# First token of three LSTMs in seven block products instead of four full ones per gate

## The chip, the cores and the metric

The kernel runs on one core of one Trainium2 chip. The metric is the time of one execution on the device in microseconds (us), as the median of several runs. The core has five engines that run side by side and meet at semaphores: TensorE (PE, matrix products, whose results land in PSUM), VectorE (DVE), ScalarE (ACT, activations and copies), GpSimd (POOL) and the queues of the DMA engines (SP issues them). Each engine takes its instructions in the order in which the program gives them, so an instruction that waits also holds up all that stand behind it.

## What is computed

The reference is a stack of four graph layers on x with 128 batches of 64 tokens and 256 channels, all in f32: a graph convolution with batch norm, a layer with two graph convolutions and four LSTMs, and two attention layers. The change lies in the LSTMs of the second layer:

```python
for p in range(1, MAX_SKIP + 1):                      # p = 1, 2, 3, 4
    nw = Tv // p                                      # 64, 32, 21, 16 windows
    wins = h[:, :nw * p, :].reshape(Bv * nw, p, Hd)   # each window has p tokens
    last = _lstm_last(Wih[p-1], Whh[p-1], bih[p-1], bhh[p-1], wins)
    h = h.at[:, jnp.arange(nw) * p + (p - 1), :].set(last.reshape(Bv, nw, Hd))

def step(carry, x_t):                                 # one token of a window
    h, c = carry
    g = x_t @ Wih.T + h @ Whh.T + bias
    i, f, gg, o = jnp.split(g, 4, axis=-1)
    c = sigmoid(f) * c + sigmoid(i) * tanh(gg)
    h = sigmoid(o) * tanh(c)
```

State and cell begin at zero, so the first token of a window needs neither Whh nor gate f: three gates (i, g, o), each of 256 output channels from 256 input channels. The LSTM with p = 1 has only that first token; "the longer LSTMs" are those with p = 2, 3 and 4.

## The kernel before

The batches go through the LSTMs in eight superchunks of 16 batches, so a superchunk has 512, 336 and 256 windows for p = 2, 3 and 4. Channels lie on the 128 partitions, windows along the columns; 256 channels are two halves. A gate is thus a product of 2 x 2 blocks of weights with 2 (input halves, k) x 2 (halves of the columns, j) blocks of data. All later tokens, and the LSTM with p = 1, already do this with seven block products in place of eight, after Strassen and Winograd: GpSimd or VectorE forms sums of data blocks (`differences`), the weights' sums were formed once, TensorE makes the seven products ("kinds" 1 to 7), and copies and adds from PSUM put them together. The first token of the longer LSTMs is done directly, with four products of the full number of columns for each gate. Gates are numbered 0, 1, 2, 3 for i, f, g, o.

The units of other work (graph convolutions of the next superchunks, residuals, norms for the attention that follows) are generators. They are advanced at marks between the parts of the LSTMs; the lists RESIDUAL, CONV, BEGUN, AHEAD, LATE give the mark for each unit. In one superchunk, marks 0 to 3 lie in the LSTM with p = 1, 4 to 7 in p = 2, 8 to 13 in p = 3, 14 to 21 in p = 4; the first two marks of a longer LSTM (4 and 5, 8 and 9, 14 and 15) lie within its first token and just behind it, and .5 stands for marks in the middle of a token.

```python
    def differences(engine, dst, b11, b12, b21, b22, third=None):
        t1, t2, t3, t4 = dst
        return [lambda: engine.tensor_tensor(t1, b12, b11, OP.subtract),
                lambda: ((third or engine).tensor_tensor(t3, b22, b12, OP.subtract),
                         engine.tensor_tensor(t2, b22, t1, OP.subtract)),
                lambda: engine.tensor_tensor(t4, b21, t2, OP.subtract)]
    # ... cut ...
    # (weight set: blocks 0-3 are the four 128x128 blocks of Wih, 8-10 three of Whh; 4-7 and 11-14 their sums)
    BLOCKS = {1: (0, 8), 2: (2, 9), 3: (7, 14), 4: (3, 10), 5: (4, 11), 6: (5, 12), 7: (6, 13)}
    # ... cut ...
    def operands_x(p, hv, name, s):
        nw, nb, inner, tokens = columns_x(p, hv)
        m = nw * nb // 2
        t = l1.tile([P, 7 * (T // 3) * NB], F32, tag="xd", name=f"xd_{name}_{s}", bufs=2)
        t = [t[:, i * m : (i + 1) * m].rearrange("p (a b) -> p a b", b=inner) for i in range(4)]
        b = {(k, j): tokens(k, s, j) for k in range(KD) for j in range(2)}
        for f in differences(nc.gpsimd, t, b[0, 0], b[0, 1], b[1, 0], b[1, 1]):
            f()
        return {5: t[0], 6: t[1], 7: t[2], 4: t[3], 1: b[0, 0], 2: b[1, 0], 3: b[1, 1]}
    # ... cut ...
        gates = l1.tile([P, 4, KD, CH], F32, tag="gates", name=f"gates_{name}", bufs=1)
        cells = l1.tile([P, KD, CH], F32, tag="cell", name=f"cell_{name}", bufs=1)
        hn = l1.tile([P, KD, CH], F32, tag="hs", name=f"hs_{name}", bufs=1)
        hd = l1.tile([P, 4, CH // 2], F32, tag="hd", name=f"hd_{name}", bufs=1)
    # ... cut ...
        dh = differences(nc.vector, [hd[:, i, :m] for i in range(4)], b[0, 0], b[0, 1], b[1, 0], b[1, 1])
        oh = {i: folded(a) for i, a in {1: b[0, 0], 2: b[1, 0], 3: b[1, 1], 4: hd[:, 3, :m],
                                        5: hd[:, 0, :m], 6: hd[:, 1, :m], 7: hd[:, 2, :m]}.items()}
        ox = {1: x1}
        banks = {(q, c): bank(f"g{q}_{name}_{c}", tag) for q, tag in ((0, "y"), (2, "z"), (3, "x"))
                 for c in range(KD)}
        def first_acts(*qs):
            for q in qs:
                for c in range(KD):
                    nc.scalar.activation(
                        columns_of(gate(q, c)),
                        natural(banks[q, c][:, :n].rearrange("p (w b) -> p w b", b=nb)),
                        AF.Tanh if q == 2 else AF.Sigmoid, bias=bs[:, q * KD + c : q * KD + c + 1])
        def first_cell(c):
            nc.vector.tensor_mul(cells[:, c, :n], gate(0, c), gate(2, c))
            nc.scalar.activation(gate(2, c), cells[:, c, :n], AF.Tanh)
        products = [(q, c, k) for k in range(KD) for q in GATES[:3] for c in range(KD)]
        for at, (q, c, k) in enumerate(products):
            if at == 6:
                yield
            nc.tensor.matmul(
                banks[q, c][:, :n].rearrange("p (w b) -> p w b", b=nb), wsets[p, q][:, 2 * k + c, :],
                hv[:, k, : (nw - 1) * p + 1 : p, :], start=(k == 0), stop=(k == KD - 1))
        first_acts(0, 2)
        first_cell(0)
        first_acts(3)
        first_cell(1)
        for c in range(KD):
            new_state(0, c, every)
            if not c:
                dh[0]()
        dh[1]()
        dh[2]()
    # ... cut ...
        class Unit:
            def __init__(self, q, s):
                self.q, self.s = q, s
                self.banks, self.of = {}, {1: "x", 6: "x", 7: "x", 4: "x", 5: "y", 2: "z", 3: "z"}
            def psum(self, kind):
                return self.banks[self.of[kind]][:, m:n] if kind == 3 else self.banks[self.of[kind]][:, :m]
            def product(self, kind, parts="xh"):
                tag = self.of[kind]
                for part in parts:
                    first = tag not in self.banks
                    if first:
                        self.banks[tag] = bank(f"{tag}{self.q}_{name}_{self.s}", tag)
                    i = "xh".index(part)
                    nc.tensor.matmul(folded(self.psum(kind)), wsets[p, self.q][:, BLOCKS[kind][i], :],
                                     (ox[self.s] if part == "x" else oh)[kind], start=first,
                                     stop=(part == "h"), skip_group_check=True)
            def copy(self, kind):
                nc.scalar.copy(gate(self.q, kind // 5, halves[kind // 5]), self.psum(kind))
            def add(self, dst, a, kind):
                nc.vector.tensor_add(gate(self.q, *dst), gate(self.q, *a), self.psum(kind))
            def c11(self):
    # ... cut ...
            def c12(self):
    # ... cut ...
        A = [Unit(q, 1) for q in (0, 2)]
        each(A, pe(5, "x"), pe(3, "x"), pe(2, "x"))
        yield
        for s in range(1, p):
            last = s == p - 1
            B = [Unit(q, s) for q in (1, 3)]
            if not last:
                ox[s + 1] = operands_x(p, hv, name, s + 1)
            each(A, pe(5, "h"), do("copy", 5), pe(1), do("copy", 1), pe(3, "h"), pe(2, "h"), pe(6), do("u4"),
                 do("c11"), do("c12"))
            each(B[:1], pe(5), do("copy", 5))
            each(A, pe(7), do("c22"), do("act", 0))
            each(B[1:], pe(5), do("copy", 5))
            each(A, pe(4), do("act", 2), do("act", 1))
    # ... cut ...
    def ahead(c):
        yield from to_pairs(c)
        stats = ln_stats(xs[c], f"n2_{c}")
        yield
        h = l1r.tile([P, NJ, D], F32, tag="g", name=f"h2_{c}", bufs=3)
        yield from apply_halves(h, xs[c], stats, f"n2_{c}")
        mid = l1r.tile([P, Q, CH * KD // Q], F32, tag="g", name=f"nm_{c}", bufs=3)
        channel_squares(mid, h)
        far2[c] = put(mid, f"n2{c}", tag=f"n2{c}", bufs=1)
        yield
    # ... cut ...
    RESIDUAL = (0, 3, 4), (2, 5, 5.5)
    CONV = (3, 4, 4, 5, 5.5, 7, 8, 9, 10, 10), (3, 4, 4, 11, 11.5, 13, 14, 15, 15.5, 17, 18, 20)
    BEGUN = (11, 11, 13, 14, 16), (17, 17.5, 21)
    FIRST = (1, 2, 3, 3, 4, 4, 5, 5.5, 7, 8, 9, 10, 10), (1, 2, 4, 5, 6, 8, 11, 11.5, 13, 14, 15, 15.5, 17, 18, 20)
    AHEAD = (4, 5, 7, 12, 14, 19), (6, 7)
    LATE = 5, 6, 8, 9
    IDLE = {5: 4, 7: 18, 9: 10, 13: 14, 15: 8}
    FINAL = (4, 5, 9.5, 10, 12, 13), (6, 7, 11.5, 14, 14, 15)
    # ... cut ...
    banks_of("psum1", x=2, y=2, z=2, ps=2)
```

## Time and profile before

| what | value |
|---|---|
| time, median of 3 runs | 1868.78 us (1867.98 to 1869.43) |
| span of the profiled execution | 1866.5 us |
| PE busy, all products | 1844.3 us, 99% |
| DVE, ACT, POOL busy | 1251.4, 1013.4, 554.1 us |
| products of the first tokens of the longer LSTMs (line L1126) | 576 records, 184.1 us |
| activations that read these products (L1113) | 144, 75.2 us |
| products of all later tokens (L1155) | 5,376 records |
| weight sets of the longer LSTMs, loaded | 96 of 960 KB |

A line of the costliest groups reads: source line, engine, operation, tile written and tiles read, shape, number of instructions, busy time, mean in ns, idle time of that engine ahead of them and what ended it. A line of the timeline reads: start in us, duration, engine, source line, operation, tiles, shape, count; in brackets the idle time ahead and the engine that ended it. An f32 product appears as two records. The end of a matmul is modelled, so distances between starts tell more of TensorE than durations. A granted clock of 0.999 shows that TensorE was not throttled.

### The profile page before, as it was taken

How to read it: one execution, taken by the hardware profiler on the slowest of the kernel's cores; microseconds unless marked ns; L12 is line 12 of the kernel's file. 1: busy time of each engine (PE TensorE's matmuls, PEld its weight loads, DVE VectorE, ACT ScalarE, POOL GpSimd, SP SyncE). 2: the span in 40 equal slices, each digit the busy share in tenths (PEclk: the TensorE clock that was granted, in tenths of full speed). 3: DMA queues.
4: the chain of work that ended last, by engine and by line, in shares of the span. 5: the costliest groups of instructions: out<-in, count | busy, mean ns of one | idle time of the engine just before them, and what ended most of it. 6: DMA issues, size and time to landing. Idle time of an engine off the chain costs nothing.

```text
span 1866.5 us, 39078 instructions
## 1 busy us (share of the span) xinstructions
PE 1844.3 (99%) x15077; PEld 1476.6 (79%) x15077; DVE 1251.4 (67%) x3150; ACT 1013.4 (54%) x2284; POOL 554.1 (30%) x704
## 2 busy tenths in 40 slices
PE   8999989999999999999999999999999999999998
PEld 6877855996897798699589689878969967777776
DVE  5767856567467666667766756766566567776776
ACT  5766635556456455555654645655565534444453
POOL 5865712123213212212322311222132114322332
PEclk9999999999999999999999999999999999999999
DMA  3223652234334433333433443343144254544433
GB/s 115 70 63 143 236 206 64 91 128 166 108 119 150 155 130 131 120 116 116 153 119 120 164 153 119 142 132 123 62 140 152 64 159 137 153 142 143 142 114 114
DMA packets 111273, 241.45 MB, mean 129 GB/s; under 512 B 11504, under 2 KB 74864, under 8 KB 111088
## 3 DMA queue, kind: packets, MB, share of 16 engines
q1 hardware_dynamic: 110192, 237.09, 37.8%
q8 instruction: 119, 1.95, 0.4%
q0 software_dynamic: 320, 1.05, 0.2%
q10 hardware_dynamic: 576, 0.82, 0.1%
q14 instruction: 66, 0.54, 0.1%
HBM read 170.50 MB, written 68.42 MB: 128 GB/s over the span
## 4 chain that ended last, share of the span: by engine, by line
PE 90%; DVE 5%; ACT 2%; issue 1%; POOL 1%; DMA 1%; SPq 0%; DVEq 0%; ACTq 0%; POOLq 0%
PE x L1155 22%; PE z L1155 11%; PE g L1126 9%; PE y L1155 6%; PE v L1580 5%; PE x L1340 4%; PE y L1340 3%; PE u L929 3%; PE v L915 3%; PE p_q L1587 3%; PE X L1776 3%; PE X L423 2%; PE X L499 2%; PE Y L423 1%; PE Y L1776 1%
## 5 line engine op out<-in xcount | busy, mean ns | idle before, releaser
L1155 PE MATMUL x<-xd,wset 128*128 128x128 f32 (+2 forms) x1152 | 255.6, 304 | 1.4 <-DVE gates L1164 1.4
L1155 PE MATMUL x<-hd,wset 128*128 128x128 f32 (+2 forms) x1152 | 254.6, 303 | 0.0
L1221 POOL TENSOR_TENSOR gates<-gates 128x512 f32<-128x512 f32 (+2 forms) x48 | 75.1, 1565 | 497.1 <-ACT gates L1084 497.1
L1084 ACT ACTIVATE gates<-gates,bias 128x256 f32<-128x256 f32 (+4 forms) x384 | 172.5, 488 | 90.3 <-DVE gates L1164 90.3
L1164 DVE TENSOR_TENSOR gates<-gates,x 128x128 f32<-128x128 f32 (+2 forms) x384 | 120.9, 321 | 149.5 <-PE x L1155 146.5
L1164 DVE TENSOR_TENSOR gates<-gates,z 128x128 f32<-128x128 f32 (+2 forms) x384 | 102.4, 318 | 146.2 <-PE z L1155 146.2
L1155 PEld LDWEIGHTS x<-xd,wset 128*128 128x128 f32 x1152 | 187.8, 191 | 7.5 <-DVE gates L1164 2.6
L1155 PEld LDWEIGHTS x<-hd,wset 128*128 128x128 f32 x1152 | 187.9, 191 | 4.9
L1126 PE MATMUL g<-hT,wset 128*128 128x256 f32 (+2 forms) x576 | 184.1, 474 | 0.1
L1126 PEld LDWEIGHTS g<-hT,wset 128*128 128x128 f32 x576 | 108.7, 190 | 68.1 <-issue 38.0
L1161 ACT COPY gates<-y 128x128 f32<-128x128 f32 (+2 forms) x192 | 54.0, 292 | 196.3 <-PE y L1155 194.4
L1155 PE MATMUL z<-hs,wset 128*128 128x128 f32 (+2 forms) x768 | 146.6, 303 | 0.2 <-DVE hs L1093 0.2
L1155 PE MATMUL z<-hT,wset 128*128 128x128 f32 (+2 forms) x768 | 146.5, 303 | 0.0
L1155 PEld LDWEIGHTS z<-hs,wset 128*128 128x128 f32 x768 | 117.3, 191 | 3.9 <-DVE hs L1093 0.6
L1155 PEld LDWEIGHTS z<-hT,wset 128*128 128x128 f32 x768 | 117.2, 191 | 3.4
L1113 ACT ACTIVATE gates<-g,bias 128x512 f32<-128x512 f32 (+2 forms) x144 | 75.2, 560 | 40.5 <-PE g L1126 39.8
L1084 ACT ACTIVATE gates<-x,bias 128x128 f32<-128x128 f32 (+2 forms) x192 | 74.8, 390 | 29.7 <-PE x L1155 26.5
L1155 PE MATMUL x<-hT,wset 128*128 128x128 f32 (+2 forms) x384 | 86.0, 306 | 0.0
L1155 PE MATMUL x<-hs,wset 128*128 128x128 f32 (+2 forms) x384 | 84.9, 303 | 0.0
L1236 ACT ACTIVATE gates<-cell 128x256 f32<-128x256 f32 (+2 forms) x144 | 55.2, 383 | 47.5 <-DVE cell L1235 47.5
L1155 PE MATMUL y<-hd,wset 128*128 128x128 f32 (+2 forms) x384 | 79.3, 309 | 0.0
L1595 POOL TENSOR_TENSOR s<-s,mx 128x256 f32<-128x256 f32 (+2 forms) x33 | 40.4, 1225 | 128.1 <-DVE mx L1594 120.3
(326 smaller groups left out, 4170.4 us busy)
## 6 DMA issues: line engine op xcount, KB each, us to landing
wset<-wfar SPq DMA_DIRECT2D x96, 960.0 KB, 6.4
hT<-far_h SPq DMA_DIRECT2D x124, 128.0 KB, 3.2
far_h<-hm SPq DMA_DIRECT2D x16, 512.0 KB, 2.8
far_n<-xs SPq DMA_DIRECT2D x16, 512.0 KB, 3.4
xs<-far_n SPq DMA_DIRECT2D x64, 128.0 KB, 4.4
far_x<-xs SPq DMA_DIRECT2D x16, 512.0 KB, 3.0
x<-far_x SPq DMA_DIRECT2D x64, 128.0 KB, 3.2
xt<-in_x_dram SPq DMA_DIRECT2D x15, 512.0 KB, 4.2
```

The lines of the kernel that those rows point to most:

```text
L423: nc.tensor.matmul(self.banks[tag][:, i * CH // 2 : (i + 1) * CH // 2], w, self.at[kind], start=first and not i, stop=True, skip_group_che ...
L915: nc.tensor.matmul(banks[m], wg0_sb[:, k, m * P : (m + 1) * P], agg[:, k, :], start=(k == 0), stop=(k == KD - 1))
L929: nc.tensor.matmul(banks[j // 2][:, j % 2, :], v[:, k, j * P : (j + 1) * P], wg1_sb[:, k, :], start=(k == 0), stop=(k == KD - 1))
L1084: nc.scalar.activation(gate(q, c, part), src, AF.Tanh if q == 2 else AF.Sigmoid, bias=bs[:, q * KD + c : q * KD + c + 1])
L1113: nc.scalar.activation(columns_of(gate(q, c)), natural(banks[q, c][:, :n].rearrange("p (w b) -> p w b", b=nb)), AF.Tanh if q == 2 else AF. ...
L1126: nc.tensor.matmul(banks[q, c][:, :n].rearrange("p (w b) -> p w b", b=nb), wsets[p, q][:, 2 * k + c, :], hv[:, k, : (nw - 1) * p + 1 : p, ...
L1155: nc.tensor.matmul(folded(self.psum(kind)), wsets[p, self.q][:, BLOCKS[kind][i], :], (ox[self.s] if part == "x" else oh)[kind], start=firs ...
L1164: nc.vector.tensor_add(gate(self.q, *dst), gate(self.q, *a), self.psum(kind))
L1221: nc.gpsimd.tensor_mul(gates[:, 0, :, :n], gates[:, 0, :, :n], gates[:, 2, :, :n])
L1340: nc.tensor.matmul(folded(ps(g, kind)), wih1[:, g, KINDS1[kind], :], right[kind], start=kind in (2, 5, 1), stop=True, skip_group_check=True)
L1580: nc.tensor.matmul(ps[:, i, :], hT[:, k, j, :], w[:, k, first : first + D], start=(k == 0), stop=(k == KD - 1))
L1776: nc.tensor.matmul(st[c, tag][:, i * CH // 2 : (i + 1) * CH // 2].rearrange("p (a n) -> p a n", n=P), w, st[c, "o7"][kind], start=first an ...
```

## The change

The first token of each longer LSTM is now done in seven block products for each gate, with half the columns each. That asks for the data sums of token 0 as well as of token 1 (`operands_x`, on GpSimd, now for both at the end of the LSTM before), and so for a third buffer of these sums. Product 1 is copied out, as is product 5; the others are added or read by an activation. Both copies follow their products in the program at once, and the activation of the first channel half follows the last add to it. One block of the weight sets, no longer read, is dropped (14 blocks in place of 15). The first product with a token's sums of kind 5 in the second token moves behind the mark, so that it stands with its partner for h. The norms of the attention for the first chunk of each superchunk move one superchunk later, as those of the second chunk already were, and other units move to other marks. The purpose is to take products from TensorE.

The diff, cut to what the working needs:

```diff
--- before.py
+++ after.py
@@ -1021,7 +1021,7 @@
-    BLOCKS = {1: (0, 8), 2: (2, 9), 3: (7, 14), 4: (3, 10), 5: (4, 11), 6: (5, 12), 7: (6, 13)}
+    BLOCKS = {1: (0, 7), 2: (1, 8), 3: (6, 13), 4: (2, 9), 5: (3, 10), 6: (4, 11), 7: (5, 12)}
     def columns_x(p, hv):
         nw, nb = hv.shape[2] // p, hv.shape[3]
@@ -1040,14 +1040,14 @@
         nw, nb, inner, tokens = columns_x(p, hv)
         m = nw * nb // 2
-        t = l1.tile([P, 7 * (T // 3) * NB], F32, tag="xd", name=f"xd_{name}_{s}", bufs=2)
+        t = l1.tile([P, 2 * CH], F32, tag="xd", name=f"xd_{name}_{s}", bufs=3)
         t = [t[:, i * m : (i + 1) * m].rearrange("p (a b) -> p a b", b=inner) for i in range(4)]
         b = {(k, j): tokens(k, s, j) for k in range(KD) for j in range(2)}
         for f in differences(nc.gpsimd, t, b[0, 0], b[0, 1], b[1, 0], b[1, 1]):
             f()
         return {5: t[0], 6: t[1], 7: t[2], 4: t[3], 1: b[0, 0], 2: b[1, 0], 3: b[1, 1]}
-    def lstm(p, hv, name, follows, x1, ending):
+    def lstm(p, hv, name, follows, ox, ending):
         nw, nb, inner, tokens = columns_x(p, hv)
@@ -1103,37 +1103,51 @@
         dh = differences(nc.vector, [hd[:, i, :m] for i in range(4)], b[0, 0], b[0, 1], b[1, 0], b[1, 1])
         oh = {i: folded(a) for i, a in {1: b[0, 0], 2: b[1, 0], 3: b[1, 1], 4: hd[:, 3, :m],
                                         5: hd[:, 0, :m], 6: hd[:, 1, :m], 7: hd[:, 2, :m]}.items()}
-        ox = {1: x1}
-        banks = {(q, c): bank(f"g{q}_{name}_{c}", tag) for q, tag in ((0, "y"), (2, "z"), (3, "x"))
-                 for c in range(KD)}
-        def first_acts(*qs):
-            for q in qs:
-                for c in range(KD):
-                    nc.scalar.activation(
-                        columns_of(gate(q, c)),
-                        natural(banks[q, c][:, :n].rearrange("p (w b) -> p w b", b=nb)),
-                        AF.Tanh if q == 2 else AF.Sigmoid, bias=bs[:, q * KD + c : q * KD + c + 1])
-        def first_cell(c):
-            nc.vector.tensor_mul(cells[:, c, :n], gate(0, c), gate(2, c))
-            nc.scalar.activation(gate(2, c), cells[:, c, :n], AF.Tanh)
-        products = [(q, c, k) for k in range(KD) for q in GATES[:3] for c in range(KD)]
-        for at, (q, c, k) in enumerate(products):
-            if at == 6:
-                yield
-            nc.tensor.matmul(
-                banks[q, c][:, :n].rearrange("p (w b) -> p w b", b=nb), wsets[p, q][:, 2 * k + c, :],
-                hv[:, k, : (nw - 1) * p + 1 : p, :], start=(k == 0), stop=(k == KD - 1))
-        first_acts(0, 2)
-        first_cell(0)
-        first_acts(3)
-        first_cell(1)
-        for c in range(KD):
-            new_state(0, c, every)
-            if not c:
-                dh[0]()
+        class First:
+            def __init__(self, q, tags):
+                self.q, self.ps = q, [bank(f"{t}{q}_{name}_{i}", t) for i, t in enumerate(tags)]
+            def psum(self, kind):
+                return self.ps[kind in (5, 3)][:, m:n] if kind in (2, 3) else self.ps[kind in (5, 3)][:, :m]
+            def product(self, kind):
+                nc.tensor.matmul(folded(self.psum(kind)), wsets[p, self.q][:, BLOCKS[kind][0], :], ox[0][kind],
+                                 start=kind in (1, 5), stop=True, skip_group_check=True)
+            def copy(self, c, j, kind):
+                nc.scalar.copy(gate(self.q, c, halves[j]), self.psum(kind))
+            def add(self, dst, a, kind):
+                nc.vector.tensor_add(gate(self.q, dst[0], halves[dst[1]]),
+                                     gate(self.q, a[0], halves[a[1]]), self.psum(kind))
+        firsts = [First(q, tags) for q, tags in ((0, "yz"), (2, "yz"), (3, "xx"))]
+        def all_first(*fs):
+            for f in fs:
+                for u in firsts:
+                    f(u)
+        def made(kind):
+            return lambda u: u.product(kind)
+        all_first(made(1), lambda u: u.copy(0, 0, 1), made(5), lambda u: u.copy(1, 1, 5))
+        yield
+        all_first(made(2), lambda u: u.add((0, 0), (0, 0), 2), made(3), made(6), lambda u: u.add((0, 1), (1, 1), 6),
+                  made(7), lambda u: u.add((1, 1), (1, 1), 7), lambda u: u.add((0, 1), (0, 1), 3), made(4),
+                  lambda u: act(u.q, 0, every, gate(u.q, 0)))
+        nc.vector.tensor_mul(cells[:, 0, :n], gate(0, 0), gate(2, 0))
+        nc.scalar.activation(gate(2, 0), cells[:, 0, :n], AF.Tanh)
+        all_first(lambda u: act(u.q, 1, halves[1], gate(u.q, 1, halves[1])),
+                  lambda u: act(u.q, 1, halves[0], u.psum(4)))
+        new_state(0, 0, every)
+        dh[0]()
+        yield "a"
+        nc.vector.tensor_mul(cells[:, 1, :n], gate(0, 1), gate(2, 1))
+        nc.scalar.activation(gate(2, 1), cells[:, 1, :n], AF.Tanh)
+        new_state(0, 1, every)
         dh[1]()
         dh[2]()
@@ -1201,14 +1215,14 @@
             return lambda u: getattr(u, f)(*a)
         A = [Unit(q, 1) for q in (0, 2)]
-        each(A, pe(5, "x"), pe(3, "x"), pe(2, "x"))
+        each(A, pe(3, "x"), pe(2, "x"))
         yield
         for s in range(1, p):
             last = s == p - 1
             B = [Unit(q, s) for q in (1, 3)]
             if not last:
                 ox[s + 1] = operands_x(p, hv, name, s + 1)
-            each(A, pe(5, "h"), do("copy", 5), pe(1), do("copy", 1), pe(3, "h"), pe(2, "h"), pe(6), do("u4"),
+            each(A, pe(5, "h" if s > 1 else "xh"), do("copy", 5), pe(1), do("copy", 1), pe(3, "h"), pe(2, "h"), pe(6), do("u4"),
                  do("c11"), do("c12"))
             each(B[:1], pe(5), do("copy", 5))
             each(A, pe(7), do("c22"), do("act", 0))
@@ -1420,7 +1433,7 @@
         def ending(p):
             if p < SKIP:
-                operands[p + 1] = operands_x(p + 1, hv, names[p + 1], 1)
+                operands[p + 1] = {s: operands_x(p + 1, hv, names[p + 1], s) for s in range(2)}
             elif sc < NCH // SUP - 1:
                 nxt = hTs[sc + 1].rearrange("p k (t b) -> p k t b", t=T)
                 operands[1] = block_sums(blocks(sc + 1, nxt), f"{sc + 1}_1")
@@ -1482,14 +1495,14 @@
-    RESIDUAL = (0, 3, 4), (2, 5, 5.5)
-    CONV = (3, 4, 4, 5, 5.5, 7, 8, 9, 10, 10), (3, 4, 4, 11, 11.5, 13, 14, 15, 15.5, 17, 18, 20)
-    BEGUN = (11, 11, 13, 14, 16), (17, 17.5, 21)
-    FIRST = (1, 2, 3, 3, 4, 4, 5, 5.5, 7, 8, 9, 10, 10), (1, 2, 4, 5, 6, 8, 11, 11.5, 13, 14, 15, 15.5, 17, 18, 20)
-    AHEAD = (4, 5, 7, 12, 14, 19), (6, 7)
-    LATE = 5, 6, 8, 9
+    RESIDUAL = (0, 3, 5.5), (2, 5, 8.5)
+    CONV = (3, 4, 5, 5.5, 7, 8, 9, 10, 10), (5, 6, 9.5, 11, 11.5, 13, 14, 15, 15.5, 17, 18, 20)
+    BEGUN = (11, 11, 14.5, 17, 19, 21), (17.5, 19, 21)
+    FIRST = (1, 2, 3, 3, 4, 4, 5, 5.5, 7, 8, 9, 10, 10), (1, 2, 4.5, 5, 6, 9.5, 11, 11.5, 13, 14, 15, 15.5, 17, 18, 20)
+    AHEAD = (6, 7), (9, 10)
+    LATE = (4.5, 5.5, 9, 9.5), (9, 11, 12, 19.5)
     IDLE = {5: 4, 7: 18, 9: 10, 13: 14, 15: 8}
-    FINAL = (4, 5, 9.5, 10, 12, 13), (6, 7, 11.5, 14, 14, 15)
+    FINAL = (6, 7, 11, 12, 15, 15.5), (9, 10, 15, 16, 17, 17.5)
     START = (0, 1, 0, 0, 0, 1, 0, 1, 1, 0, 0, 1, 1, 0, 1, 2, 2)
     tc.no_sync_barrier()
@@ -1526,8 +1539,6 @@
                     todo.setdefault(n, []).append(unit)
-            if sc > 1:
-                units(LATE[:1], aheads[sc * SUP - 3])
             if sc < last:
                 for i in range(SUP):
                     units((CONV if sc else FIRST)[i], convs[(sc + 1) * SUP + i])
 ... cut: the block dropped from the weight sets; block_sums gets the same new buffers; both places that call units with LATE ...
```

## The prediction

> **What bounds the kernel now.** I read the page first: engine totals, chain, groups.
>
> ```profile
> span 1866.5 us, 39078 instructions
> ## 1 busy us (share of the span) xinstructions
> PE 1844.3 (99%) x15077; PEld 1476.6 (79%) x15077; DVE 1251.4 (67%) x3150; ACT 1013.4 (54%) x2284; POOL 554.1 (30%) x704
> ...
> PE 90%; DVE 5%; ACT 2%; issue 1%; POOL 1%; DMA 1%; SPq 0%; DVEq 0%; ACTq 0%; POOLq 0%
> ...
> L1126 PE MATMUL g<-hT,wset 128*128 128x256 f32 (+2 forms) x576 | 184.1, 474 | 0.1
> ```
>
> TensorE is the bound, and the products to be replaced (L1126, tile g) are 184 us of its time. Busy time does not say whether PE has slack, since ends of matmuls overlap and are modelled. So next I read the timeline of PE by start times, in the first tokens of one superchunk with p = 2, 3 and 4 (each product is two records, so x24 is 12 products):
>
> ```profile
> 603.17 5.31 PE L1126 MATMUL g<-hT,wset 128*128 128x512 f32 x12
> 608.41 1.16 PE L214 MATMUL agg_b<-adjt_bd,cv 64*64 64x64 f32 x64
> 609.50 5.42 PE L1126 MATMUL g<-hT,wset 128*128 128x512 f32 x12
> 614.76 1.03 PE L1155 MATMUL y<-xd,wset 128*128 128x256 f32 x4
> ...
> 645.82 6.94 PE L1126 MATMUL g<-hT,wset 128*128 128x336 f32 x24
> 652.60 0.73 PE L1155 MATMUL y<-xd,wset 128*128 128x168 f32 x4
> 653.17 1.30 PE L1155 MATMUL z<-hT,wset 128*128 128x168 f32 x8
> 654.40 1.16 PE L214 MATMUL agg_c<-adjt_bd,cv 64*64 64x64 f32 x64
> 655.49 0.84 PE L1155 MATMUL y<-hd,wset 128*128 128x168 f32 x4
> ...
> 690.53 5.34 PE L1126 MATMUL g<-hT,wset 128*128 128x256 f32 x24
> 695.71 0.61 PE L1155 MATMUL y<-xd,wset 128*128 128x128 f32 x4
> ```
>
> Start to start, a product of 336 columns takes (652.60-645.82)/12 = 0.565 us, one of 256 takes (695.71-690.53)/12 = 0.432. Other rows give 0.858 for 512, 0.285 for 168 (656.17, 656.45, 656.74) and 0.223 for 128. That is 1.65 ns a column plus about 11 ns, and no gap: the rows stand end to end. PE has almost no slack to hide a new wait in, and almost no old wait to lose. From one superchunk's start to the next is 153.5 us, and the starts show about 1.3 us of it lost in waits.
>
> **What the Trainium skill says.** "TensorE: Matmul & The Clock Gate", section "Back-to-back issue gap", makes the gap of warm matmuls N/2.4 + 2.5 ns. Per record our 112, 143, 216 and 429 ns are twice the N/2.4 part plus about 5 ns for these f32 products: the linear shape agrees, so narrow products cost no penalty here, though each weight load shows as 191 ns. "VectorE: DVE Perf Modes", section "The TRN2 errata", gives an f32 tensor_tensor as (N+151)/0.96 ns: 691, 424, 332 and 291 ns for 512, 256, 168, 128. The trace has 687, 420, 327 and 283, so of every small add about 155 ns is fixed. "PSUM — Partial Sum Buffer", section "PSUM bank collisions raise a hardware error", asks that PSUM be guarded by bank and quadrant, not by address. No run shows the error itself, but the changed program's waits follow that: product 2, which writes the second half of bank y, waits for ScalarE's copy of the first half.
>
> **The change, part by part.** First, PE. Before, per superchunk: 12 products of 512, 336, 256 columns = 12 x (0.858+0.565+0.432) = 22.26 us. After: 7 x 3 = 21 products of half the width = 21 x (0.432+0.285+0.223) = 19.74. Saved: 2.5 us a superchunk, 20 us in eight, 1.1% of the time. This is the ceiling of the gain.
>
> Second, the other engines. The seven products must be added up. For each p VectorE gets 12 adds from PSUM (0.42, 0.33, 0.28 us): 12 x 1.03 = 12.4 us a superchunk on top of 104.4 busy of 153.5. ScalarE loses 6 wide activations and gets 6 copies, 3 wide and 6 half ones, about 9 us on top of 86.4. GpSimd gets 4 differences for each p (0.73, 0.54, 0.45): 7 us on top of 37. None becomes the bound by load. Weight sets shrink from 960 to 896 KB; no wait for them stands in the chain, so nothing from that.
>
> Third, latency, where PE waits in order. I followed the changed order of instructions with the durations of the trace. From a product's end to the add's start is 0.27 us, other hand-overs are about 0.06.
>
> (a) Start of a token. The gates tile has one buffer, so the first copy waits for the previous LSTM's last state on VectorE, and product 2 waits for that copy. Before, products of the first input half took long enough to cover it.
>
> ```profile
> 604.63 0.65 DVE L1350 TENSOR_TENSOR gates<-gates 128x512 f32<-128x512 f32 x1
> 605.20 0.68 DVE L1356 TENSOR_TENSOR hT<-hs,gates 128x512 f32<-128x512 f32 x1
> 606.05 1.20 DVE L1356 TENSOR_TENSOR hT<-cell,gates 128x512 f32<-128x512 f32 x1 [0.16 <-ACT gates L1353]
> ...
> 646.10 0.99 DVE L1099 TENSOR_TENSOR hT<-gates 128x256 f32<-128x256 f32 x2
> ```
>
> For p=2 the state is there at 607.25. The aggregation (1.16) now stands ahead of the token, then products 1 and 5 take 6 x 0.432, so PE would be at product 2 at 603.17+1.16+2.6 = 606.9. The copy ends at 607.3+0.37, so PE starts at 607.7: 0.8 us lost. For p=3 and 4 a block of 3.4 us (u, v) stands ahead of the token; states come at 647.0 and 690.95, products 2 are due at 645.82+1.71 = 647.5 and 690.53+1.34 = 691.9: nothing lost.
>
> (b) Inside: products 6, 7 and 4 of a gate share one bank half, so each waits for the add of the one before, with two other gates between. For p=4, three products are 0.67 us and one round trip is 0.22+0.27+0.28+0.06 = 0.83: 0.16 lost twice, 0.3. For p=3 0.1 each, 0.2. For p=2 three products are 1.3: nothing.
>
> (c) End: the next token's product 5 needs bank y, which ScalarE frees only after three wide gates, one tanh, three half gates and then the half gate from that bank. For p=3: the last product 4 starts near 651.7, adds of product 3 end 651.9 to 652.5, three gates (0.5 apart) 653.5, tanh 654.1, four half gates 655.5. PE needs 1.14 for its four ready products and 1.2 for the aggregation, so it is there at 654.3: 1.2 lost. For p=2 and 4, v or u (3.4 us) stands there and covers it. Also for p=3, VectorE does the moved norm statistics (2.1 us) just ahead of the next token's adds: up to 0.7 more, which I count half.
>
> Sum of new waits a superchunk: 0.8 + 0.2 + 1.2 + 0.35 + 0.3 = 2.85 us. The last superchunk has no convolutions to fill waits of p=2 and p=4: some 3 us more. The norms that leave p=4 take statistics and activations out of the way of an old wait of 0.4 us there (below), which should go in most superchunks: -2.5 us.
>
> ```profile
> 712.51 0.49 PE L1155 MATMUL x<-xd,wset 128*128 128x128 f32 x2 [0.24 <-DVE gates L1164]
> ```
>
> Total: -20 + 8 x 2.85 + 3 - 2.5 = +3 us by this count. Each wait is worked out from VectorE and ScalarE running strictly in order; my errors are of 0.5 us a place, or some 6 to 10 us together, and my count takes every coincidence at its worst, though the units were moved (marks 5.5, 8.5, 14.5) so as to stay behind the first state. I therefore take 4 us off: **1868 us**.
>
> **Rivals.** The first: the waits are hidden, and all 20 us arrive, giving 1849. For it: PE's rows are so dense that the author clearly places fillers well, and only p=3 lacks one. Against it: the aggregation is 1.2 us, and the chain of (c) is 3.5. The second: VectorE becomes the bound in p=3 and p=4, because 12 adds more, slowed by GpSimd, fall into 4 us. For it: two tensor_tensor of 336 columns took 1.62 us instead of 1.0 at 651.68, while GpSimd worked there until 652.9. Against it: VectorE's load goes only from 68% to 76%. That would cost 1 to 1.5 us more a superchunk: 1878. The third: the transfers of weights, smaller now, start earlier and help. No wait for them is visible, so 0.
>
> **Range and chances.** The best case is 1849 plus a little, as some wait is sure: 1852. The worst has both later rivals' costs and a poor last superchunk: 1883. Over 2% faster (1831) is beyond the ceiling of the PE count; over 2% slower (1906) needs 7 us of waits a superchunk. So 0.01, 0.96, 0.03.
>
> **What would show it.** PE's product rows should have starts 0.432, 0.285, 0.223 apart; 504 products in place of 288. A gap ahead of product 2 for p=2 released by ScalarE's copy; a gap ahead of bank y's product in the second token of p=3, about 1.2 us, released by ScalarE; small ones inside p=4 released by VectorE's adds. Superchunks near 153.7 us apart. If they are 151 apart, (a) and (c) were hidden and I am wrong by some 20 us; if 155 or more, VectorE's queue is the cause.

## The result, and the profile after

The changed kernel takes **1896.66 us** (median of 4 runs, 1896.2 to 1897.3) against 1869.11 us (1867.98 to 1869.78) of the kernel before on the same chip. The ratio is 1.0148 with a 95% interval of 1.0131 to 1.0166: 27.5 us slower. I had predicted 1868 us with a range of 1852 to 1883; the time lies above it, on the side of the waits.

The page of the kernel after, the lines that answer to those shown of before (engine totals, chain by engine, and the group with the most idle time ahead of it on TensorE):

```profile
span 1894.5 us, 40708 instructions
...
PE 1840.2 (97%) x15509; PEld 1515.4 (80%) x15509; DVE 1325.8 (70%) x3438; ACT 1053.0 (56%) x2500; POOL 600.1 (32%) x800
...
PE 79%; DVE 11%; ACT 5%; issue 2%; POOL 2%; DMA 1%; SPq 0%; DVEq 0%; ACTq 0%; POOLq 0%
...
L1169 PE MATMUL x<-xd,wset 128*128 128x128 f32 (+2 forms) x1152 | 256.6, 304 | 12.4 <-ACT gates L1175 10.1
```

By the page TensorE is busy 4 us less (busy time counts modelled ends; the starts give more, see the table of terms below), and the span is 28 us longer. In the chain TensorE falls from 90% to 79%: the end is now set in part by VectorE and ScalarE. Neither is full; VectorE went from 67% to 70%. The last row is the first surprise: 10.1 us of waits in the *later* tokens' products (L1169, in the code of before L1155), of which the change only moves the first ones of the second token, for ScalarE's copies L1175.

The timeline of TensorE in superchunk 2, the first tokens with p=2, 3 and 4 and the tokens behind them (in square brackets the idle time ahead of a row and what ended it):

```profile
612.23 1.13 PE L1116 MATMUL y<-hT,wset 128*128 128x256 f32 x4 [0.56 <-ACT gates L1120]
...
657.58 1.16 PE L214 MATMUL agg_c<-adjt_bd,cv 64*64 64x64 f32 x64
659.62 0.52 PE L1169 MATMUL y<-xd,wset 128*128 128x168 f32 x2 [0.89 <-ACT gates L1084]
...
665.20 0.55 PE L1169 MATMUL x<-xd,wset 128*128 128x168 f32 x2 [0.21 <-DVE gates L1178]
...
736.07 0.46 PE L1169 MATMUL x<-xd,wset 128*128 128x128 f32 x2 [1.40 <-ACT gates L1175]
```

The first three waits stand where the prediction put them. Taken start to start, as the excess over the usual distance of two records, they are 0.72, 1.04 and 0.37 us. The fourth, 1.56 us in the last token of p=4, I had not seen.

The same by the matmuls' starts (first product of an LSTM to first product of the next, us), for superchunk 2, which stands for the steady ones, and for the last:

| | p=1 and 2 | p=3 | p=4 | superchunk 2 | superchunk 7 | behind the LSTMs |
|---|---|---|---|---|---|---|
| before | 60.68 | 44.71 | 48.13 | 153.52 | 143.06 | 371.1 |
| after | 60.27 | 45.98 | 49.25 | 155.49 | 153.35 | 375.4 |

The whole difference of the two profiled spans, 28.0 us, is: start -0.5, superchunk 0 +3.5, superchunks 1 to 6 +10.4, superchunk 7 +10.3, and the attention stage behind the LSTMs, which the change does not touch, +4.3.

### The profile page after: what moved, and what is told of

It is laid out like the page before. It is cut to its first block, busy times and chain, and to the rows that moved or that the text cites. A ratio compares the mean times of both kernels' runs of the same rounds, so it can differ in the third digit from the quotient of the medians.

```text
span 1894.5 us, 40708 instructions
## 1 busy us (share of the span) xinstructions
PE 1840.2 (97%) x15509; PEld 1515.4 (80%) x15509; DVE 1325.8 (70%) x3438; ACT 1053.0 (56%) x2500; POOL 600.1 (32%) x800
## 4 chain that ended last, share of the span: by engine, by line
PE 79%; DVE 11%; ACT 5%; issue 2%; POOL 2%; DMA 1%; SPq 0%; DVEq 0%; ACTq 0%; POOLq 0%
PE x L1169 20%; PE z L1169 10%; PE v L1592 5%; PE y L1169 5%; PE y L1116 4%; PE u L929 3%; PE v L915 3%; PE y L1353 3%; PE X L1788 3%; PE p_q L1599 3%; PE x L1353 2%; PE X L423 2%; PE x L1116 2%; PE X L499 2%; PE z L1116 1%
## 5 line engine op out<-in xcount | busy, mean ns | idle before, releaser
L1084 ACT ACTIVATE gates<-gates,bias 128x256 f32<-128x256 f32 (+4 forms) x528 | 237.8, 495 | 204.0 <-DVE gates L1178 109.0
L1169 PE MATMUL x<-xd,wset 128*128 128x128 f32 (+2 forms) x1152 | 256.6, 304 | 12.4 <-ACT gates L1175 10.1
L1169 PE MATMUL x<-hd,wset 128*128 128x128 f32 (+2 forms) x1152 | 254.6, 303 | 0.0
L1169 PEld LDWEIGHTS x<-xd,wset 128*128 128x128 f32 x1152 | 187.2, 191 | 21.5 <-issue 12.2
L1169 PEld LDWEIGHTS x<-hd,wset 128*128 128x128 f32 x1152 | 187.7, 191 | 5.0
L1169 PE MATMUL z<-hs,wset 128*128 128x128 f32 (+2 forms) x768 | 146.3, 303 | 0.0
L1169 PE MATMUL z<-hT,wset 128*128 128x128 f32 (+2 forms) x768 | 146.2, 303 | 0.0
L1175 ACT COPY gates<-y 128x128 f32<-128x128 f32 (+2 forms) x192 | 52.9, 289 | 131.8 <-PE y L1169 125.5
L1169 PEld LDWEIGHTS z<-hs,wset 128*128 128x128 f32 x768 | 116.9, 191 | 3.6 <-DVE hs L1093 0.4
L1169 PEld LDWEIGHTS z<-hT,wset 128*128 128x128 f32 x768 | 117.1, 191 | 3.3
L1084 ACT ACTIVATE gates<-x,bias 128x128 f32<-128x128 f32 (+2 forms) x216 | 84.5, 391 | 31.5 <-PE x L1169 28.3
L1169 PE MATMUL y<-xd,wset 128*128 128x128 f32 (+2 forms) x384 | 81.7, 305 | 9.8 <-ACT gates L1084 9.8
L1169 PE MATMUL x<-hT,wset 128*128 128x128 f32 (+2 forms) x384 | 85.8, 305 | 0.0
L1169 PE MATMUL x<-hs,wset 128*128 128x128 f32 (+2 forms) x384 | 84.9, 303 | 0.0
L1169 PE MATMUL y<-hd,wset 128*128 128x128 f32 (+2 forms) x384 | 82.5, 307 | 0.0
L313 POOL TENSOR_TENSOR xd<-hT 128x128 f32<-128x128 f32 (+2 forms) x72 | 41.9, 582 | 128.1 <-DVE hT L1095 105.7
L1594 ACT COPY v<-v 128x512 f32<-128x512 f32 x64 | 37.1, 581 | 73.1 <-PE v L1592 73.1
```

What stands on the lines that cost most here:

```text
L1084: nc.scalar.activation(gate(q, c, part), src, AF.Tanh if q == 2 else AF.Sigmoid, bias=bs[:, q * KD + c : q * KD + c + 1])
```

## The experiments

No variant leaves work out. Two theories stood against each other first. **Q, queue order:** the units that were moved (norms, convolutions, residuals) now stand ahead of something urgent in an engine that works strictly in order. **B, block chain:** the copies and adds of the block products cost the time wherever the units stand.

### Products alone, moves alone

*products*: the changed kernel with all marks as before.

```diff
-    RESIDUAL = (0, 3, 5.5), (2, 5, 8.5)
-    BEGUN = (11, 11, 14.5, 17, 19, 21), (17.5, 19, 21)
-    LATE = (4.5, 5.5, 9, 9.5), (9, 11, 12, 19.5)
+    RESIDUAL = (0, 3, 4), (2, 5, 5.5)
+    BEGUN = (11, 11, 13, 14, 16), (17, 17.5, 21)
+    LATE = 5, 6, 8, 9                # CONV, FIRST, AHEAD, FINAL likewise
```

> The block products alone: the changed kernel with every unit of the norms, convolutions and residuals back at the marks of the kernel before. Theory Q (the moved units stand in the way: the norm application at mark 19 sits in ScalarE's queue ahead of two copies that TensorE waits for, 1.56 us in each of seven superchunks, and a late transfer of wqv_sb at the end, 1 us): without the moves these 12 us go, but the old wait of 0.4 us in p=4 comes back and some statistics stand ahead of the new adds, together up to 1 us a superchunk; 1885 to 1892. Theory B (the block products' copies and adds cost the time themselves, wherever the units stand): 1897 or more, because the moves were made to relieve them.

*moves*: the kernel before with the marks of after, and a half mark in its first tokens:

```diff
             new_state(0, c, every)
             if not c:
                 dh[0]()
+                yield "a"
```

> The moves alone: the kernel before, four full products a gate, with the marks of the changed kernel (its first token gives up at the same half marks). Theory Q: the wait of some 1.5 us in the last token of p=4 appears here too in seven superchunks, plus the late wqv_sb, less the old 0.4 us wait: 1875 to 1881. Theory B: 1864 to 1870, as the moves by themselves cost nothing.

Measured: products 1966.24 us, ratio 1.0525 (1.0507 to 1.0543); moves 1880.19 us, ratio 1.0060 (1.0045 to 1.0075). *products* refutes Q's 1885 to 1892; it fits B only because B was left open at the top, as neither theory had a cost of nearly 100 us in it. The moves save 70 us of that, so B has a large part in it. *moves* lies in Q's range (1875 to 1881) and not in B's. By themselves the moves cost 11.7 us: 7.5 of it in p=4 of superchunks 0 to 5, 2.0 in the attention stage, 1.6 in p=2 of superchunk 0 (a fall of TensorE's clock, last section). The timeline of TensorE in *moves* has the same wait, of the same size, with full products in the first tokens:

```profile
734.13 0.46 PE L1156 MATMUL x<-xd,wset 128*128 128x128 f32 x2 [1.40 <-ACT gates L1162]
```

So this wait belongs to the moves and not to the block products. ScalarE's timeline of the kernel after, at that place, shows why:

```profile
734.36 1.09 ACT L196 ACTIVATE cv<-xs,nmr_b,rstd_b 128x256 f32<-128x256 f32 x2 [1.09 <-DVE nmr_b L194]
735.36 0.40 ACT L1175 COPY gates<-y 128x128 f32<-128x128 f32 x2
```

The norm application (L196) moved from mark 16 to mark 19. It waits 1.09 us for nmr_b, which VectorE makes only after the state's operands (at 734.17), and works 1.09 us more. All that time the copies L1175, whose products were done by 733, stand behind it, and TensorE's next product needs the bank that they free. The Trainium skill, "Perfetto Trace Analysis", section "Tensor Engine Instruction (MATMUL, LD_WEIGHTS)", says that ScalarE, VectorE and GpSimd are strict FIFO; the rows agree, as no copy overtakes the waiting application.

### The norm application at other marks

*apply18* puts it into the middle of the token before, *apply1925* four ScalarE instructions later, behind the copies:

```diff
-    BEGUN = (11, 11, 14.5, 17, 19, 21), (17.5, 19, 21)
+    BEGUN = (11, 11, 14.5, 17, 18, 21), (17.5, 19, 21)       # apply18
+    BEGUN = (11, 11, 14.5, 17, 19.25, 21), (17.5, 19, 21)    # apply1925
...
-            each(A, pe(5, ...), do("copy", 5), pe(1), do("copy", 1), pe(3, "h"), ...)
+            each(A, pe(5, ...), do("copy", 5), pe(1), do("copy", 1))
+            yield "b"                                         # mark .25
+            each(A, pe(3, "h"), ...)
```

> The changed kernel with one mark moved: the first half of the norm application of the even chunk at mark 18 instead of 19, so that it stands in ScalarE's queue behind other work and not ahead of the last token's copies. Theory Q: the wait of 1.56 us in p=4 goes from seven superchunks, 1885 to 1888. Theory B: the copies are late for ScalarE's load as such, the wait stays or turns up a token earlier, 1894 to 1898.

> The changed kernel, with the norm application that stood at mark 19 put four ScalarE instructions later: behind the copies of the last token's first two products instead of ahead of them (a new mark there). Theory Q (order in ScalarE's queue alone): the wait of 1.56 us in p=4 goes completely from seven superchunks and nothing else changes: 1885 to 1887. Rival L (ScalarE's load in that token): the copies stay late or another wait of 0.5 us or more comes in the same token: 1889 or more.

Measured: apply18 1890.80 us (ratio 1.0119, 1.0103 to 1.0134), apply1925 1886.94 us (1.0097, 1.0082 to 1.0112). At mark 18 the wait goes, but 0.40 and 0.19 us come into the token before. At 19.25 p=4 falls from 49.25 to 47.62 us and no wait takes its place: 1.62 us in each of superchunks 0 to 5, 9.7 us. (I had written seven superchunks; the unit exists in six.) ScalarE's timeline of *apply1925*, the copies first and the application in a gap of its queue:

```profile
730.21 0.41 ACT L1175 COPY gates<-y 128x128 f32<-128x128 f32 x2
...
732.58 1.09 ACT L196 ACTIVATE cv<-xs,nmr_b,rstd_b 128x256 f32<-128x256 f32 x2 [1.46 <-DVE nmr_b L194]
```

### Step (a): the gates buffer

*hdcopy*: the first three copies go to the tile hd, which is free then, so that they need not wait for the gates tile.

```diff
-    all_first(made(1), lambda u: u.copy(0, 0, 1), ...
+    all_first(made(1), First.early, ...      # nc.scalar.copy(hd[:, gate, :m], psum(1)); the add reads it there
```

> The changed kernel, with the first copies (product 1 of the three gates) going to a tile that is free at that time (hd) instead of to the gates tile, which the previous LSTM's last state still reads; the adds take them from there. If that buffer is what delays product 2, its wait of 0.72 us in p=2 goes in seven superchunks, and 1.6 us in the last one: 1889 to 1892. If the second copies (product 5, still to the gates) take its place ahead of product 3, at most half of that: 1893 to 1896.

Measured: 1891.00 us (1.0119, 1.0104 to 1.0134). That lies in the range that I had named for the buffer alone, but by luck: p=1 and 2 fall only from 60.27 to 59.88, and the row of TensorE says why: product 2 now waits for its *operand*, the very state that had held the buffer.

```profile
611.78 0.45 PE L1116 MATMUL y<-hT,wset 128*128 128x256 f32 x1 [0.20 <-DVE hT L1375]
```

So of the 0.72 us the buffer was 0.37 and the data the rest. The LSTMs take 4.2 us less from first to last product; 2.0 us more come from the attention stage (373.4 instead of 375.4 us), which the edit does not touch and on which I come below, and the LSTMs start 0.5 us later.

### Step (c): the end of a first token, p=3

*swap*: bank y is freed three activations earlier.

```diff
-        all_first(lambda u: act(u.q, 1, halves[1], gate(u.q, 1, halves[1])),
-                  lambda u: act(u.q, 1, halves[0], u.psum(4)))
+        all_first(lambda u: act(u.q, 1, halves[0], u.psum(4)),
+                  lambda u: act(u.q, 1, halves[1], gate(u.q, 1, halves[1])))
```

> The changed kernel with ScalarE's last six activations of a first token in another order: the three that read PSUM (product 4) ahead of the three that read the gates from SBUF. If the chain at the token's end is as I worked it out for p=3 (bank y comes free only behind three half activations of about 0.35 us each), the wait of 1.04 us in p=3 of each superchunk and the 1.96 us in p=2 of the last one go: 7 to 9 us less, 1887 to 1890. If another bank or operand becomes last at once (bank x, which the third gate frees), 2 us or less: 1894 to 1897.

Measured: 1896.18 us (1.0147, 1.0132 to 1.0162), and p=3 as long as ever (45.95). TensorE does start bank y without the wait, and stands eight products later for the recurrent state, in the timeline of *swap*:

```profile
661.46 0.84 PE L1169 MATMUL z<-hs,wset 128*128 128x168 f32 x4 [0.42 <-DVE hs L1093]
```

The bank was the first of two waits that end at the same time, so freeing it is worth nothing: what bounds the boundary is the chain to the second half of the state (adds, gates, tanh, cell). To see that chain's price I took it out of p=3 alone. Full products need one more weight block. *p3direct* loads it into hd just in time, *p3w* an LSTM ahead into the tile that p=3's block operands would have taken:

```diff
-    {s: operands_x(p + 1, hv, names[p + 1], s) for s in range(2)}
+    {s: operands_x(p + 1, hv, names[p + 1], s) for s in range(p == 2, 2)}
...
+    if p == 2: direct = l1.tile(..., tag="xd"); nc.sync.dma_start(direct, w1far[...][:, 1])     # p3w
+    if direct: the twelve full products and six activations of the kernel before, for p = 3
```

> The changed kernel with the first token of p=3 alone back to four full products a gate, in all superchunks (the weight block that this needs comes into the hd tile, which is free then); p=2 and p=4 keep the block products. If my step (c) is right that p=3 loses by the block products because its token boundary has only an aggregation to fill it: p=3 falls from 45.97 to some 44.8 us in seven superchunks and by some 4 us in the last: 1883 to 1887. If the state itself is as late with full products, or the moved statistics are what costs there: 1892 or more.

> The changed kernel with the first token of p=3 alone in four full products a gate, the missing weight block loaded a whole LSTM ahead into the tile that its block operands would have taken, the products in the order of the kernel before. If step (c) is right: p=3 takes 44.7 to 44.9 us instead of 45.97 in seven superchunks and some 43 instead of 45.9 in the last: 1896.7 less 10 to 11: 1885 to 1887. If p=3 is as long with full products (the marks cost it): 1893 or more.

Measured: p3direct 1894.69 us (1.0138, 1.0123 to 1.0153), which tells nothing, as its weights came late (TensorE waits 0.35 us for them in superchunk 2) and its products stood in another order; p3w 1887.43 us (1.0103, 1.0086 to 1.0120), just above what was expected. By stage p3w is clear: p=3 falls from 45.98 to 44.88 us, in the last superchunk from 45.86 to 43.12. TensorE's timeline of *p3w*:

```profile
656.87 1.16 PE L214 MATMUL agg_c<-adjt_bd,cv 64*64 64x64 f32 x64
657.96 0.55 PE L1207 MATMUL y<-xd,wset 128*128 128x168 f32 x2
```

With full products bank y's product follows the aggregation at once (657.96). The block products lose 1.1 us net in p=3, that is 1.9 us of waits against 0.8 us of TensorE time saved.

*p3marks* moves the statistics that stand ahead of the second token's adds:

```diff
-    LATE = (4.5, 5.5, 9, 9.5), (9, 11, 12, 19.5)
+    LATE = (4.5, 5.5, 9, 9.5), (9.5, 11, 12, 19.5)
```

> The changed kernel with the norm statistics of the odd chunk at mark 9.5 instead of 9, behind the second token's first adds on VectorE and not ahead of them. If they are what delays those adds (0.37 us at x<-xd in p=3), 2 to 2.6 us go: 1894 to 1895. If the adds are late anyway, or the statistics delay the next ones as much: 1896 to 1898.

Measured: 1894.30 us (1.0137, 1.0122 to 1.0152); p=3 45.49 instead of 45.98. The statistics were worth 0.49 us, between the 0.35 that I had counted and the 0.7 that I had halved.

### The last superchunk

The waits of TensorE in superchunk 7 of the kernel after (us in total, times, longest us):

```profile
PE y L1169 <- ACT gates L1084: 3.7, 3, 1.8
PE y L1116 <- ACT gates L1120: 2.6, 3, 1.5
PE x L1169 <- ACT gates L1175: 1.4, 2, 1.2
...
```

Here no convolution fills a token's end, and steps (c) and (a), the first two rows, come back for p=2, 3 and 4. *lastdirect* uses full products in this superchunk only (the weight blocks come into the convolutions' tile, which is free by then).

```diff
+    if sc == NCH // SUP - 1: direct = ...     # first tokens of p = 2, 3, 4 as in the kernel before
```

> The changed kernel, with the first tokens of the last superchunk alone done in four full products a gate as before; the first seven superchunks keep the block products. If the chain of copies and adds is what costs there, where no convolution stands beside it to fill waits: the last superchunk falls from 153.4 us to some 144 us, 1886 to 1889. If the moved units cost it: 1893 or more.

Measured: 1886.48 us (1.0095, 1.0080 to 1.0110), and the last superchunk takes 143.51 instead of 153.35 us. The same view of *lastdirect*, complete:

```profile
PE x L1207 <- ACT gates L1213: 1.4, 2, 1.2
PE x L1207 <- DVE gates L1216: 0.5, 1, 0.5
```

*tail* takes up the first wait of the attention stage, 0.97 us for the load of wqv_sb, by putting the squares of the odd chunk earlier in the last superchunk:

```diff
-    units(LATE[i], aheads[(sc - 2) * SUP + i])
+    units(LATE[i] if sc < last or not i else (9, 11, 12, 16), aheads[(sc - 2) * SUP + i])
```

> The changed kernel with the last superchunk's squares of the odd chunk at mark 16 instead of 19.5. If the put of these squares, ahead of the load of wqv_sb in the queue of transfers, is what makes TensorE wait when the attention stage begins: the wait of 1.1 us there goes, the stage after the LSTM takes 374 instead of 375.4 us: 1895 to 1896. If not: 1896.5 to 1897.5.

Measured: 1896.47 us (1.0147, 1.0132 to 1.0162). The wait goes (374.2 instead of 375.4 us behind the LSTMs), but the squares on VectorE make the last superchunk 0.9 us longer: nothing gained.

### Versions that keep what pays

*combo1* is apply1925, hdcopy, lastdirect and tail together. *combo2* adds full products for p=3 through hd (and for p=2 of the first superchunk); *combo3* is combo1 with p=3 as in p3w; *combo4* adds p3marks; *combo5* also moves one statistics unit of the first superchunk:

```diff
-    FIRST = (1, 2, 3, 3, ...
+    FIRST = (1, 1, 3, 3, ...
```

> The three edits of this batch together, and in the last superchunk the squares of the odd chunk at mark 16 instead of 19.5 (so that their transfer no longer stands ahead of that of wqv_sb: 1 us). If the three add up (11 + 6 + 10 + 1, less the part of the second that the third takes): 1868 to 1873. If they share waits: 1875 or more.

> The combination before with p=3 direct in every superchunk, and p=2 of the first superchunk direct too (there GpSimd's differences for the block products stand behind a norm's rsqrt, 2.4 us): block products only where a convolution product fills the token's end. If gains add up: 1872.6 less 7 x 1.1 less 1.3: 1862 to 1866, faster than both kernels. If p=3 keeps its length, or the transfer into hd is late: 1870 or more.

> The first combination (norm application behind the copies, first copies to hd, last superchunk with full products, its squares at mark 16; 1872.6 us) with p=3 in full products in every superchunk: block products in p=2 and p=4 of seven superchunks only. If gains add up, 7 x 1.1 us less: 1864 to 1866, faster than the kernel before by 0.1 to 0.25%. If the wait of p=3 comes back in another token: 1869 or more.

> The same, with the norm statistics of the odd chunk at mark 9.5 instead of 9. With full products in p=3 VectorE has no adds of a first token there and the statistics delay little: 0 to 1 us less than the same without it. If they still stand ahead of the second token's adds: 2 to 3 us less.

> The same again, and in the first superchunk the norm statistics of the even chunk at mark 1 instead of 2, so that GpSimd's rsqrt for them no longer stands ahead of the differences for p=2's block products. If that order is the wait of 2.4 us of p=2 in the first superchunk: 1 to 2.4 us less. If VectorE gets in the way in p=1 instead: 0 or more.

| | us | ratio to before, 95% interval | superchunk 2 | superchunk 7 |
|---|---|---|---|---|
| combo1 | 1872.57 | 1.0021 (1.0014 to 1.0029) | 153.33 | 144.46 |
| combo2 | 1881.16 | 1.0069 (1.0052 to 1.0086) | 154.00 | 150.17 |
| combo3 | 1866.65 | 0.9991 (0.9985 to 0.9998) | 152.36 | 144.45 |
| combo4 | 1866.45 | 0.9990 (0.9984 to 0.9997) | 152.35 | 144.46 |
| combo5 | 1866.83 | 0.9992 (0.9984 to 1.0001) | 152.35 | 144.45 |
| combo6 | 1865.04 | 0.9982 (0.9975 to 0.9989) | 152.37 | 142.94 |

combo1 adds up as expected. combo2 failed by its means: the block for hd came 1.0 us late, and another order of products made TensorE wait for hT, 1.89 us in the last superchunk and 2.96 us in p=2 of the first. combo3 is just faster than the kernel before (by 1.4 us, which is no more than the attention stage varies by itself, see below). combo4 gains nothing over it, as expected with full products in p=3. combo5 takes 3.6 us from p=2 of the first superchunk and gives 3.9 to p=1: the statistics now stand ahead of p=1's adds on VectorE, and TensorE waits 2.34 us for those.

In superchunk 7 of combo4 TensorE still waits 1.4 us for copies (ACT, L1219) and 1.3 us for adds (DVE, L1222), with norm units at marks 11, 15 and 17, at the start of tokens. *combo6* puts these units behind the copies:

```diff
-    FINAL = (6, 7, 11, 12, 15, 15.5), (9, 10, 15, 16, 17, 17.5)
+    FINAL = (6, 7, 11.25, 12, 15.25, 15.5), (9, 10, 15.25, 16, 17.25, 17.5)
-    ... else (9, 11, 12, 16)
+    ... else (9.5, 11.25, 12, 16)
```

> The combination with full products in p=3 and the last superchunk and the statistics at 9.5 (1866.45 us), with the norm applications and statistics of the last superchunk that stand at marks 11, 15 and 17 put at 11.25, 15.25 and 17.25, behind the copies of that token. If the same head-of-line order is what is left there: the last superchunk 142 to 143 us instead of 144.46, 1864 to 1865.5. If those waits have another cause: 1866 to 1867.

Measured: 1865.04 us (1863.76 to 1865.64, 18 runs) against 1868.28: 0.9982 (0.9975 to 0.9989). The last superchunk falls by 1.5 us (142.94 from 144.46): the waits for copies go, those for adds (0.97 and 0.62 us by the starts) stay, so their cause was another: *tail* has the same two (0.97 and 0.63) where *after* and *lastdirect* have a single one of 0.68 and 0.67, so they come with the squares that tail put earlier. This is the fastest version: block products for p=2 and p=4 in seven superchunks, full ones elsewhere. From first to last product its LSTMs take 5.5 us less than those of before (1215.6 against 1221.1 us), of which the attention stage gives 1.8 back (372.9 against 371.1). Its page:

```profile
span 1862.0 us, 40089 instructions
...
PE 88%; DVE 7%; ACT 2%; POOL 2%; issue 1%; DMA 0%; DVEq 0%; SPq 0%; ACTq 0%; POOLq 0%
```

## Why the prediction was wrong

The steps of the sum, predicted and measured (us; measured from the starts of the matmuls in the two profiles):

| term | predicted | measured | from |
|---|---|---|---|
| TensorE's work saved | -20 | -19.8 | 24 x (0.429 + 0.2825 + 0.216) - 42 x (0.216 + 0.143 + 0.112) = 2.48 a superchunk |
| new waits less the old one, superchunks 0 to 6 | +17.5 | +21.7 | 14.0 longer, + 7 x 2.48, less the next row |
| norm application ahead of the copies | 0 | +9.7 | apply1925: 6 x 1.62 |
| last superchunk | +5.9 | +12.8 | 10.3 + 2.48 |
| start and attention stage | 0 | +3.8 | -0.5 + 4.3 |
| taken off, "as my count takes every coincidence at its worst" | -4 | 0 | |
| sum | -0.6 | +28 | |

**Right.** The saving (2.5 a superchunk) and nearly every wait of the steady superchunks: (a) 0.8 predicted, 0.72 found; (b) 0.16 twice in p=4, found 0.17 and 0.19; (c) 1.2, found 1.04; the statistics 0.35, found 0.37. Net of the norm application, p=4 is 47.62 in apply1925 against 48.13 before: 0.51 us shorter, so its 0.50 us of saved work arrive and the old wait of 0.40 pays for the new ones of 0.36. Of (c) the size was right and the cause half: bank y is where TensorE stood, but swap shows that the state behind it is as late. Of (a) half was the buffer, as I had it; the rest was the data itself. (A slip on which nothing rests: the records stand 2 to 5 ns above twice N/2.4, not all "about 5".)

**Wrong, first: "The norms that leave p=4 take statistics and activations out of the way of an old wait".** I counted the moved units only where they left and, on VectorE, where they stood ahead of adds. I did not follow ScalarE's queue at the marks to which they went. The unit at mark 19 is that step's miss: 9.7 us, shown by moves (it is there with full products) and by apply1925 (it goes with four instructions' difference in order).

**Wrong, second: "The last superchunk has no convolutions to fill waits of p=2 and p=4: some 3 us more."** The mechanism was right and the term mis-sized: 12.8 us in all instead of 5.9. lastdirect gives 9.8 us of the 10.3 back, so the block products' own chains cost it. I had lent p=3 the wait of the steady superchunks, but with full products it is 2.7 us shorter there too (p3w: 43.12 against 45.86). Part of the last superchunk's waits was again order in ScalarE's queue: a wait of 1.38 us for the copies L1175 in p=3 stands in after and, for the same copies, in lastdirect (1.37) and combo4 (1.38), and combo6 takes it away.

**Wrong, third: the 4 us taken off.** Nothing in the profile spoke for it. The steady waits came out as counted, with 0.6 us a superchunk more on average; most of that surplus is in superchunks 0 and 6.

**The first superchunk** lost 3.5 us: 1.75 in p=2, 0.6 in p=3, 1.2 in p=4 (the norm application's 1.6 less what p=4 gains). In p=2 GpSimd's queue has an order of the same kind, in the timeline of after:

```profile
295.93 0.23 POOL L99 TENSOR_SCALAR rstd_b<-mv_b 128x4 f32<-128x4 f32 x1 [4.22 <-DVE mv_b L160]
...
297.26 0.94 POOL L313 TENSOR_TENSOR xd<-hT 128x256 f32<-128x256 f32 x1
```

A norm's rsqrt waits for VectorE, and the difference that a block product needs waits behind it; TensorE then waits 2.24 us for xd. But here too two waits end together: the aggregation behind waits for the application of that same norm (cv) in any case. TensorE's timeline of *tail*, which is the same here, then of before:

```profile
298.63 1.13 PE L1116 MATMUL z<-xd,wset 128*128 128x256 f32 x4 [2.23 <-POOL xd L313]
...
300.49 1.94 PE L214 MATMUL agg_b<-adjt_bd,cv 64*64 64x64 f32 x64 [0.30 <-ACT cv L196]
```

```profile
300.67 1.94 PE L214 MATMUL agg_b<-adjt_bd,cv 64*64 64x64 f32 x64 [1.22 <-ACT cv L196]
```

From the token's first product (293.96 and 294.13) to the aggregation it is 6.53 us in tail and 6.54 in before, so the wait for xd by itself costs nothing. What costs is that the block products leave less work ahead of that point (2.6 us in place of 5.2) and more behind it (6.5 in place of 5.2): 1.3 us. The other 0.4 us is a fall of TensorE's clock that after shows here and tail does not (last section). combo5 moved the norm's statistics and got a wait in p=1 instead, so how to order this is open.

**The rivals.** That all waits are hidden (1849) is refuted. That VectorE becomes the bound (1878) is not what happened: in superchunk 2 it is busy 73% of the time, TensorE's waits for its adds in p=3 and p=4 there are 0.37, 0.17 and 0.19 us, and the largest single wait came from ScalarE's order. But the sentence "if 155 or more, VectorE's queue is the cause" was wrong: superchunks were 155.5 apart, and it was ScalarE's queue.

**Open.** The attention stage is 4.3 us longer. The wqv_sb wait is 1 of it, and 0.8 lies behind the last product. Another 2 are waits of TensorE for "issue", that is, for nothing the profile shows, inside its runs of small products; from the lists of waits, first after, then before:

```profile
PE p_q L1599 <- DMA wqv_sb<-wqv_far: 1.0, 1, 1.0
...
PE s L1867 <- issue: 2.1, 2, 1.2
```

```profile
PE s L1855 <- issue: 0.2, 1, 0.2
```

They sit at the same two products in after, p3marks and tail (near 1719 and 1856 us) and elsewhere in programs of another length (hdcopy once, 0.9 us; combo6 twice, 1.5 us). So they seem to go with the program's layout and not with its data flow; what makes them no run here shows. In *moves*, with full products, the stage is already 2.0 us longer (a single wait of 1.5 us for "issue"). A difference of 1 or 2 us between two of these kernels can come from this alone, and one of 0.4 to 1.7 us from a fall of the clock (last section).

## What to carry to other kernels

When work is moved to make room on one engine, read the queue of every in-order engine at the place it goes to: a unit that is itself waiting, put one place ahead of an instruction that frees a PSUM bank, cost half of what the products saved. A narrower product that needs copies and adds paid here only where other TensorE work stood at the token's end (p=2 and p=4 with a convolution product), so decide it place by place. And where two waits end together, freeing the one the profile names gains nothing; find the second before you spend effort on the first.

## What the runs showed of the hardware

In *products* a wait is paid twice. The timeline of VectorE, then of TensorE, in p=2 of superchunk 2:

```profile
634.60 0.16 DVE L194 SCALAR_TENSOR_TENSOR nmr_b<-mv_b,rstd_b 128x4 f32<-128x4 f32 x1 [2.30 <-POOL rstd_b L100]
...
635.99 0.75 DVE L1123 TENSOR_TENSOR gates<-gates,y 128x256 f32<-128x256 f32 x2
```

```profile
636.55 2.04 PE L1116 MATMUL y<-xd,wset 128*128 128x256 f32 x4 [4.20 <-DVE gates L1123]
638.39 1.06 PE L1116 MATMUL x<-xd,wset 128*128 128x256 f32 x2
639.25 1.91 PE L1116 MATMUL y<-xd,wset 128*128 128x256 f32 x4
...
641.58 1.03 PE L1116 MATMUL y<-xd,wset 128*128 128x256 f32 x4
```

The adds stand behind a norm that waits for GpSimd's rsqrt, and TensorE idles 4.20 us. Then its products are at half speed for 5 us: 0.86 us from 638.39 to 639.25 for one product of 256 columns, against 0.43 from 641.58 on.

The trace also has the granted clock. In *products* it is one half in stretches of 3.41 us or twice that (634.50 to 641.33 is one), and these begin at whole multiples of 3.413 us from each other: 252.21, 395.57, 470.66 and 559.41 are 42, 22 and 26 of them apart. The windows below are laid on that grid. Behind the comma stands TensorE's busy time, and the third number from the end is the granted clock. First *products* around the wait shown, then around one of 3.41 us in superchunk 0 (304.89 to 308.30):

```profile
631.09:634.50 3.41, 1.26 (x6) 0.76 (x4) 1.21 (x3) 0.00 (x0) 3.25 (x5) 1.00 0.10 30
634.51:637.91 3.40, 1.36 (x3) 1.17 (x4) 2.51 (x7) 2.08 (x4) 0.06 (x1) 0.50 0.29 114
...
303.41:306.82 3.41, 1.48 (x7) 0.95 (x5) 0.39 (x2) 0.00 (x0) 1.12 (x2) 1.00 0.49 149
306.82:310.24 3.42, 1.94 (x9) 1.62 (x10) 3.11 (x8) 0.00 (x0) 0.00 (x0) 1.00 0.00 0
```

Then the wait of 2.2 us for xd, the same in *after* and in *tail*:

```profile
295.44:298.85 3.41, 1.17 (x5) 0.72 (x6) 3.38 (x7) 1.03 (x2) 2.18 (x3) 1.00 0.28 115
298.86:302.27 3.41, 3.41 (x69) 2.58 (x67) 0.56 (x2) 2.82 (x8) 2.77 (x4) 0.50 0.40 123
```

```profile
296.87:300.28 3.41, 1.56 (x6) 1.06 (x6) 2.94 (x5) 1.07 (x2) 2.18 (x3) 1.00 0.38 154
300.28:303.70 3.42, 3.15 (x70) 2.61 (x71) 1.15 (x2) 3.25 (x10) 3.34 (x6) 1.00 0.58 157
```

The Trainium skill, "TensorE: Matmul & The Clock Gate", section "What's actually happening", says that TensorE falls to half its clock after an idle window of about 3.4 us. The length of the stretches agrees, but the window need not be idle throughout: the clock fell behind windows with 1.26 and 1.17 us of work and stayed behind those with 1.48 and 1.56. So the length of a wait alone does not decide, but also how it lies on the grid. The 3.41 us wait, split between two windows, cost no clock; the wait for xd was followed by a fall in 7 of the 15 kernels that have it. Nor is busy time the whole measure. In *moves* the clock fell behind a window with 2.12 us of work (298.14 to 301.55, most of it the small aggregation products, and a wait of 1.23 us); before has the same wait (1.22 us) and no fall. What exactly is counted these runs do not show.

A fall cost 0.44 us in p=2 of superchunk 0 of after (46.47 against 46.03 in tail) and 1.65 in moves (46.37 against 44.72 in before). In *products* 51 us of TensorE's work lie in half-clock stretches; my estimate from that is 25 of its 98 us. That is one part of why the marks of before are so much dearer with block products; the waits themselves, 39 us for adds (L1123) and 16 for GpSimd's rsqrt at these products, are the larger.
